# Steps of two attention rows instead of one in a fused window-attention and Fourier kernel

## The chip, the cores and the metric

The kernel runs on one core of one Trainium2 chip, in one launch, in float32. The metric is device time of one execution in microseconds (us).

Engines are named as the profile names them: PE is TensorE (matmuls), PEld its weight loads, DVE is VectorE, ACT ScalarE, POOL GpSimd, SP the engine that issues DMAs.

## The reference

Two layers are computed on 32 images of 56 x 56 tokens with 128 channels. Each adds its result to its input, and each works on a group norm of it (32 groups of 4 channels).

```python
def layer0(x):                       # shifted-window attention: window 7, shift 3, 4 heads of 32
    xs  = roll(x, (-3, -3));  win = windows_of_49_tokens(xs)
    q, k, v = split(win @ w_qkv.T)
    a   = softmax(q @ k.T * 32**-0.5 + rel_bias + shift_mask)
    return roll(unwindow(a @ v @ w_proj.T + b_proj), (3, 3))

def layer1(x):                       # Fourier layer: 32 modes along the width, 32 along the height
    xy = idct(einsum('bixy,ioy->boxy', dct(x, width )[..., :32], w0))
    xx = idct(einsum('bixy,ioy->boxy', dct(x, height)[..., :32], w1))
    return relu((xx + xy) @ W1 + b1) @ W2 + b2      # 128 -> 512 -> 128

x = x + layer0(group_norm(x))
x = x + layer1(group_norm(x))
```

(The text above is the reference in short form; names are shortened, the arithmetic is not.)

## The kernel before

An image has eight rows of windows, with eight windows of 49 tokens in each. The attention of one image runs beside the Fourier layer of the image before it and the feed-forward (the last two matmuls of the layer) of the one before that. The whole order of instructions on each engine is written by hand.

The parts of the kernel use TensorE in four tilings: full, 128x128 (q, k, transposes, projection, feed-forward), 128x64 (v, transforms, mix), 64x64 (scores, modes back), 64x32 (values). One cycle handles one row and goes through them:

```python
def attn_v(im, i, r):                # 128x64; 16 matmuls as the profile counts them
    pv = attn_bank()
    for w in (0, 2, 1, 3, 4, 6, 5, 7):
        nc.tensor.matmul(pv[...], lhsT=im.xw[i][...], rhs=im.w[:, 2*C:3*C], ...)
    nc.scalar.copy(v_sb[r % 3]..., pv)

def attn_scores(im, i, r):           # 64x64; 32 matmuls in the profile, then two adds on VectorE
    ps = [attn_bank(), attn_bank()]
    ...
    nc.vector.tensor_tensor(a[...], ps[hp][...], bm[...], ALU.add)

def attn_transpose(im, i, r):        # full
    for hf in range(2):
        pt = attn_bank()
        ...                          # four transposes into the bank
        if hf: nc.scalar.copy(aT[:PW, :, :PW], src)
        else:  nc.vector.tensor_copy(aT[:PW, :, :PW], src)

def attn_values(im, i, r):           # 64x32; 64 matmuls in the profile; reads aT and v
    po = [attn_bank(), attn_bank()]
    ...                              # then bias adds po -> oT, on VectorE and ScalarE

# [cut: statistics, transforms, mix, modes back, feed-forward]

for cycle in ...:                    # one row a cycle
    full_first(cycle, norm)          # transposes of row r-2, q and k of row r, feed-forward in, divide of row r-1
    if (cycle - CONV_BEGIN) % NWR != 3:
        quarters(cycle)              # scores of row r, modes back
        attn_max(cycle)
        half_columns(cycle)          # v of row r, transforms or mix
        eighths(cycle)               # values of row r-2
    else:                            # the same in another order
        ...
    full_last(cycle, norm)           # feed-forward out, exp of row r, projection of row r-2
```

## Time and profile before

| | before |
|---|---|
| median of 3 runs | 3698.61 us (3693.87 to 3700.42) |
| TensorE busy | 98% of the span |
| time per image in the steady part | 112.7 us |

How to read the views. The *page* gives busy time per engine, and the chain of work that ended last. The *waits of TensorE* list what it stood idle for: the line that waited, the releaser, the sum in us, how often, and the longest. "Issue" there is idle time in which it waited for nothing that the profile shows. The *timeline* gives start, duration, engine, line and instruction; a bracket at the end is the idle time before it and its releaser. A matmul record's end is modelled, so blocks are compared by their starts; and since idle time is counted from that modelled end, a row of the waits can give too little.

The line numbers move by one between the kernels. The parts on TensorE are:

```
                  before  after            before  after
image transposes  L259    L260   values     L444    L445
q / k             L321/8  L322/9 project    L486    L487
v                 L353    L354   transform  L595    L596
scores            L375    L376   mix        L629    L630
transposes        L419    L420   modes back L668    L669
                                 ff in/out  L711/31 L717/37
```

The waits of TensorE in the kernel before:

```profile
PE pa L259 <- DMA xl<-in_x_dram: 11.2, 2, 6.9
PE pa L375 <- DVE k L341: 8.3, 6, 1.8
...
PE pa L444 <- issue: 2.1, 4, 1.2
...
```

Nothing is large and no wait recurs for every image: there are 32 images, and the counts are 2, 6 and 4.

### The profile page before, as it was taken

Reading aid. Unit: us, or ns where it says so; the run is one execution under the profiler, and the core shown is the slowest. Engines: PE = TensorE matmul, PEld = TensorE weight load, DVE = VectorE, ACT = ScalarE, POOL = GpSimd, SP = SyncE. Lnnn points to the kernel's source line nnn. Section 1 sums busy time; section 2 is a strip of 40 time slices with the busy share of each in tenths; the row PEclk is TensorE's granted clock in tenths of the full one; section 3 lists DMA queues with packets and bytes.
Section 4 is the critical chain, followed back from the end, with each engine's and each line's share of the span. In section 5 each row is a group of like instructions: output and inputs, shape, how many; then the busy total and the mean of one; then the engine's idle time right before and its main releaser. Section 6 shows DMA issues by size and latency. Waiting matters only on the chain.

```text
span 3694.8 us, 139935 instructions
## 1 busy us (share of the span) xinstructions
PE 3628.2 (98%) x61440; PEld 2966.3 (80%) x61440; DVE 2185.3 (59%) x4577; ACT 2151.0 (58%) x3915; POOL 1372.0 (37%) x1421
## 2 busy tenths in 40 slices
PE   6899999999999999999999999999999999999998
PEld 5678888888888887888888888878888888888886
DVE  6655666655665556665556656556655566565641
ACT  4555566655656655566556566555665565565553
POOL 5333343333334333433333343334333333433321
PEclk9999999999999999999999999999999999999999
DMA  4333434343434334334334344343344343333332
GB/s 112 93 102 104 116 93 109 107 111 101 113 95 114 108 105 113 96 105 110 108 102 113 95 111 108 105 113 100 101 112 108 101 115 97 108 107 106 95 107 89
DMA packets 687777, 388.93 MB, mean 105 GB/s; under 512 B 40479, under 2 KB 658112, under 8 KB 686912
## 3 DMA queue, kind: packets, MB, share of 16 engines
q1 hardware_dynamic: 686557, 379.65, 37.6%
q8 instruction: 484, 7.93, 0.9%
q14 instruction: 125, 1.02, 0.1%
q10 hardware_dynamic: 611, 0.32, 0.0%
HBM read 218.29 MB, written 161.48 MB: 103 GB/s over the span
## 4 chain that ended last, share of the span: by engine, by line
PE 93%; DVE 4%; DMA 1%; SPq 1%; ACT 1%; issue 0%; POOL 0%; ACTq 0%; POOLq 0%; DVEq 0%
PE pc L731 21%; PE pc L711 18%; PE pa L353 7%; PE pc L629 6%; PE pc L595 6%; PE pa L375 6%; PE pa L419 5%; PE pa L486 5%; PE pc L668 5%; PE pa L328 5%; PE pa L444 4%; PE pa L321 4%; PE pa L259 2%; DVE st L270 1%; DVE a L383 1%; DVE mx L393 1%
## 5 line engine op out<-in xcount | busy, mean ns | idle before, releaser
L408 POOL TENSOR_TENSOR a<-a,rs 128x784 f32<-128x784 f32 x256 | 389.9, 1523 | 1231.0 <-DVE rs L407 962.6
L731 PE MATMUL pc<-wff,hid 128*128 128x128 f32 (+1 forms) x6400 | 778.6, 279 | 0.9 <-ACT hid L719 0.7
L731 PEld LDWEIGHTS pc<-wff,hid 128*128 128x128 f32 (+1 forms) x6400 | 731.1, 189 | 21.1 <-issue 2.1
L711 PE MATMUL pc<-xf,wff 128*128 128x512 f32 (+2 forms) x1792 | 713.1, 540 | 0.9 <-ACT z L637 0.9
L719 ACT ACTIVATE hid<-pc,b1sb 128x512 f32<-128x512 f32 (+2 forms) x896 | 536.6, 635 | 97.8 <-PE pc L711 94.2
L711 PEld LDWEIGHTS pc<-xf,wff 128*128 128x128 f32 x1792 | 337.0, 190 | 301.7 <-issue 229.5
L394 POOL TENSOR_TENSOR a<-a,mx 128x784 f32<-128x784 f32 x256 | 389.4, 1521 | 451.6 <-DVE mx L393 450.4
L740 DVE TENSOR_TENSOR res<-pc,res 128x512 f32<-128x512 f32 (+2 forms) x256 | 143.6, 571 | 597.0 <-issue 273.9
L427 ACT COPY aT<-pa 113x452 f32<-113x452 f32 x256 | 137.8, 538 | 457.6 <-PE pa L419 457.5
L274 POOL TENSOR_TENSOR xl<-xl,bproj 112x384 f32<-112x384 f32 (+1 forms) x256 | 291.9, 1142 | 248.7 <-PE pa L259 248.7
L383 DVE TENSOR_TENSOR a<-pa,bm 128x392 f32<-128x392 f32 x512 | 259.6, 550 | 199.3 <-PE pa L375 199.1
L341 DVE TENSOR_SCALAR k<-pa,heads,bqkv 128x392 f32<-128x392 f32 x246 | 168.6, 685 | 275.3 <-ACT k L333 275.3
L475 DVE TENSOR_SCALAR oT<-pa,bqkv 128x98 f32<-128x98 f32 (+2 forms) x768 | 171.0, 279 | 266.4 <-PE pa L444 266.4
L400 ACT ACTIVATE a<-a 128x784 f32<-128x784 f32 x256 | 223.1, 872 | 168.9 <-POOL a L394 168.5
L360 ACT COPY v<-pa 128x512 f32<-128x512 f32 x256 | 152.9, 597 | 278.4 <-PE pa L353 278.4
L701 POOL TENSOR_TENSOR res<-res,b2sb 128x512 f32<-128x512 f32 (+2 forms) x256 | 263.5, 1035 | 101.4 <-DMA res<-scr 91.3
L375 PEld LDWEIGHTS pa<-k,q 64*64 64x64 f32 x8192 | 184.0, 132 | 137.8 <-DVE rs L407 68.2
L353 PE MATMUL pa<-wn,xw 128*64 128x128 f32 x4096 | 281.8, 280 | 3.7 <-DVE a L383 3.7
L353 PEld LDWEIGHTS pa<-wn,xw 128*64 128x64 f32 x4096 | 219.8, 137 | 51.6 <-issue 17.2
L393 DVE TENSOR_REDUCE mx<-a 128x16 f32<-128x784 f32 x256 | 247.6, 967 | 5.7
L405 DVE TENSOR_REDUCE sm<-a 128x16 f32<-128x784 f32 x256 | 245.9, 961 | 4.9 <-ACT a L400 4.9
L419 PE MATMUL pa<-ident,a 113*113 113x113 f32 x2048 | 248.2, 264 | 0.7 <-POOL a L408 0.7
(89 smaller groups left out, 5896.8 us busy)
## 6 DMA issues: line engine op xcount, KB each, us to landing
zscr<-z SPq DMA_DIRECT2D x512, 112.0 KB
htok<-scr SPq DMA_DIRECT2D x256, 196.0 KB
zT<-zscr SPq DMA_DIRECT2D x192, 256.0 KB
res<-scr SPq DMA_DIRECT2D x160, 256.0 KB
out_dram<-res SPq DMA_DIRECT2D x128, 256.0 KB
scr<-xl SPq DMA_DIRECT2D x128, 224.0 KB
xl<-in_x_dram SPq DMA_DIRECT2D x32, 784.0 KB
xl<-in_x_dram SPq DMA_DIRECT2D x32, 672.0 KB
```

Of the source, the lines that this page charges most:

```text
L274: nc.gpsimd.tensor_tensor(piece, piece, bproj.unsqueeze(1).to_broadcast([TC, n1 - n0, C]), ALU.add)
L353: nc.tensor.matmul(pv[hs, j * C : (j + 1) * C], lhsT=im.xw[i][:, w * WT : w * WT + JP], rhs=im.w[:, 2 * C : 3 * C], start=True, stop=True,)
L375: nc.tensor.matmul(ps[hp][HALVES[e], pr * 2 * WT : (pr + 1) * 2 * WT], lhsT=q[cs, w * WT : w * WT + JP], rhs=k_sb[cs, :, w], start=True, s ...
L383: nc.vector.tensor_tensor(a[:, 2 * hp : 2 * hp + 2, :, 0:WT].rearrange("p u w j -> p w u j"), ps[hp][:, :RT].rearrange("p (w u j) -> p w u ...
L393: nc.vector.tensor_reduce(mx, a3, axis=AX.X, op=ALU.max)
L394: nc.gpsimd.tensor_tensor(a3, a3, mx.unsqueeze(2).to_broadcast([P, 2 * NWR, WT]), ALU.subtract)
L408: nc.gpsimd.tensor_tensor(a3, a3, rs.unsqueeze(2).to_broadcast([P, 2 * NWR, WT]), ALU.mult)
L419: nc.tensor.transpose(pt[:PW, h * P : h * P + PW], a[:PW, h, 2 * hf : 2 * hf + 2].rearrange("p w j -> p (w j)")[:, :PW], ident[:PW, :PW],)
L701: nc.gpsimd.tensor_tensor(res[:m, c0:c1], res[:m, c0:c1], b2sb[:m].unsqueeze(1).to_broadcast([m, c1 - c0, C]), ALU.add,)
L711: nc.tensor.matmul(ph[:, :n], lhsT=wff1[:, f * P : (f + 1) * P], rhs=xff[:, t0 : t0 + n], start=True, stop=True,)
L719: nc.scalar.activation(hf[:, :n], ph[:, :n], AF.Relu, bias=b1sb[:, f : f + 1])
L731: nc.tensor.matmul(pf[:m, c * C : (c + 1) * C], lhsT=im.hid[f][:, c * P : c * P + m], rhs=wff2[:, f], start=(f == 0), stop=(f == NF - 1),)
```

## The change

Its intent: two rows of attention per step, so that blocks of one tiling stand together and TensorE changes its tiling five times per two rows instead of eight. For that, the softmax of a row is a step (two rows) long, the transposes stand one step after the scores, the width modes are transformed back before the height modes, and the feed-forward has eight even groups in place of seven uneven ones. q, k and the transposed scores get further buffers; the buffers of the scores go from three to two.

```diff
-FF_GROUPS = (HB, HB, HB, HB, 320, 256, HB)
-FF_AT = (7, 8, 9, 10, 12, 13, 14)
+FF_GROUPS = (3 * P,) * 7 + (7 * JP,)
-CONV_BEGIN = NWR + 2
+CONV_BEGIN = NWR // 2 + 1
 [cut: buffers; k_sb[r % 2], q_sb[r % 2], a_sb[r % 2]; im.aT[i]; width copied, height added]
-    def full_first(cycle, norm):
-    def half_columns(cycle):
-    def quarters(cycle):
-    def eighths(cycle):
-    def full_last(cycle, norm):
+    def step(g):
+        prev, cur, b, i = rows(g - 1), rows(g), *divmod(g, STEPS)
 [cut: groups 6 and 7 of the next image; first part of its norm]
+        for im, d in conv:
+            if d >= FF_BEGIN:
+                ff_in(im, 2 * (d - FF_BEGIN))
+        for im, j, r in prev:
+            if once("divide", r):
+                attn_divide(r)
+        sums = []
+        for im, j, r in rows(g - 2):
+            if once("sums", r):
+                sums.append(attn_sums(im, j))
+                next(sums[-1])
+        for im, j, r in cur:
+            attn_qk(im, j, r, False)
+        if norm:
+            next(norm)
+        for k in sums:
+            next(k)
 [cut: first half of the statistics, loads]
+        for im, d in conv:
+            if d >= FF_BEGIN:
+                ff_out(im, 2 * (d - FF_BEGIN))
+                ff_in(im, 2 * (d - FF_BEGIN) + 1)
+        for im, d in conv:
+            if d == 0:
+                next(im.stats)
+        if norm:
+            next(norm)
+        if i == STEPS - 2:
+            groups((0, 1, 2))
+        for im, j, r in prev:
+            attn_transpose(im, j, r)
+        for im, j, r in prev[:1]:
+            attn_values(im, j, r)
+        for k in range(2):
+            for im, d in conv:
+                if d in (2, 3):
+                    modes_back(im, d == 2, k)
+        for im, j, r in cur:
+            attn_scores(im, j, r)
 [cut: modes_back of groups 2 and 3; maxima; transforms and mix]
+        for im, j, r in cur:
+            attn_v(im, j, r)
+        for im, j, r in prev[1:]:
+            attn_values(im, j, r)
+        for im, j, r in cur:
+            attn_exp(r)
+        for im, d in conv:
+            if d >= FF_BEGIN:
+                ff_out(im, 2 * (d - FF_BEGIN) + 1)
+        for im, j, r in prev:
+            attn_project(im, j)
 [cut: groups 3 to 5 of the next image; last part of its norm]
```

An image takes four such steps. I call the one with d = 0 the statistics step, the one with the next image's groups 0 to 2 the group step, and the one with the next image's norm the norm step.

## The prediction

> **What bounds the kernel now.** I read the page first (busy shares, slices, chain), then the busy time of each engine in the steady part, then the waits of TensorE, and last the timeline of TensorE, block by block.
>
> From the page and from the windows view (us of the window, then PE, PEld, DVE, ACT, POOL busy, clock):
>
> ```profile
> PE 3628.2 (98%) x61440; PEld 2966.3 (80%) x61440; DVE 2185.3 (59%) x4577; ACT 2151.0 (58%) x3915; POOL 1372.0 (37%) x1421
> ...
> PE 93%; DVE 4%; DMA 1%; SPq 1%; ACT 1%; issue 0%; POOL 0%; ACTq 0%; POOLq 0%; DVEq 0%
> ...
> 130.00:3500.00 3370.00, 3353.98 (x57453) 2748.83 (x57454) 2040.36 (x4257) 2000.43 (x3646) 1278.06 (x1316) 1.00 0.39 106
> ```
>
> TensorE is busy 98% of the span and 99.5% of the steady part, at full clock; it carries 93% of the chain. In its wait list nothing exceeds 11.2 us (the first image's load); all waits for another engine together come to some 55 us, nearly all in the first 130 us and the last 90. So the time is the sum of TensorE's work, and only two things can move it: less TensorE time, or a new wait of TensorE.
>
> A busy engine is not an engine at its peak, so I looked at how long the same block takes before different successors (timeline: start, duration, what):
>
> ```profile
> 1812.58 0.82 PE L328 MATMUL pa<-xw,wn 128*128 128x392 f32 x2
> 1813.24 3.60 PE L711 MATMUL pc<-xf,wff 128*128 128x512 f32 x8
> 1816.77 0.90 PE L375 MATMUL pa<-k,q 64*64 64x98 f32 x32
> 1817.60 1.09 PE L353 MATMUL pa<-wn,xw 128*64 128x128 f32 x16
> 1818.53 1.80 PE L595 MATMUL pc<-dct_h,htok 112*64 112x64 f32 x56
> ...
> 1841.39 0.90 PE L375 MATMUL pa<-k,q 64*64 64x98 f32 x32
> 1842.12 1.71 PE L668 MATMUL pc<-idcth,zT 64*64 64x112 f32 x64
> ...
> 1886.90 1.09 PE L353 MATMUL pa<-wn,xw 128*64 128x128 f32 x16
> 1887.92 0.81 PE L444 MATMUL pa<-aT,v 49*32 49x49 f32 x64
> ```
>
> Read starts, not durations (ends are modelled). The 32 score matmuls (64 rows x 64 columns) take 1817.60-1816.77 = 0.83 us when a block of another tiling follows, and 1842.12-1841.39 = 0.73 us when one of the same tiling follows. The 16 value projections (128x64) take 0.93 us before the transform of the same tiling and 1.02 us before the 49x32 block. So **a change of tiling costs about 0.10 us**, with no gap that the idle column would show.
>
> [...]
>
> **The change part by part.**
>
> *Tiling changes.* Before, each row of attention passes through full array, 64x64, 128x64, 64x32 (in one phase in another order): four changes a row, eight per two rows. Afterwards a step of two rows goes full array, 64x32 (values of the first row), 64x64, 128x64, 64x32, full array: five. Counted over the whole instruction order of TensorE, with each matmul put to its tiling, there are 1110 changes before and 726 after: 384 fewer. The sum is 384 x 0.10 = **38 us less** (1.0%), all of it on the path, since TensorE is the path. Per image of 113.2 us (from one image load's issue to the next) that is 12 x 0.10 = 1.2 us.
>
> *TensorE's other work.* Counts of transposes, projections, scores, values, transforms, mixes are equal. The feed-forward goes from seven groups (five of 512) to eight (seven of 384, one of 448): the same 3136 columns and the same 100 second-stage matmuls an image; 4 more wide matmuls, at a few ns each of fixed cost. Zero. The 64-token rest, with its two changes of tiling, stays.
>
> *Other engines.* Width now comes first and is copied out half by ScalarE, half by VectorE; height is added by VectorE alone. VectorE gains 128 copies of about 0.6 us (L684's mean 596 ns), 75 us, to 61%; ScalarE loses about as many. VectorE's load sits in the step that adds height: 2.4 divide + 2.4 sums + 1.4 keys + 1.2 transposes out + 1.7 values + 4.5 height + 2.0 scores + 1.9 maxima + 2.4 residuals and projection = about 20 us in a step of some 25 us. Laid beside TensorE's order, the bank that the value projection needs comes free about 0.9 us ahead. No wait, but thin.
>
> *The softmax.* Transposes now come one step after the scores, and within the step behind two feed-forward inputs, one output and two rows of queries and keys: 2 x 2.58 + 2.69 + 2.63 = 10.5 us. The divide needs two sums and reciprocals on VectorE (2 x 1.22) and two products on GpSimd (2 x 1.52), about 5.5 us after the step begins. Hidden.
>
> *What the shorter distance exposes.* The first row's values now come right behind the transposes: TensorE needs 16 x 0.099 = 1.6 us for both rows, and the copy of the first quarter (615 ns on VectorE) must be done by then. Usually it is. Not where VectorE has something ahead of it:
> - In the step that begins the Fourier part, the group statistics stand just ahead of the copies:
>
> ```profile
> 1898.77 0.33 PE L537 MATMUL pa<-tot,gmean 112*128 112x64 f32 x2
> ...
> 1900.13 0.55 POOL L566 TENSOR_TENSOR rstd<-ve,mhalf 128x1 f32<-128x1 f32 x1 [7.78 <-DVE ve L562]
> 1900.71 0.16 DVE L568 SCALAR_TENSOR_TENSOR shift<-ms,rstd 128x1 f32<-128x1 f32 x1 [0.66 <-POOL rstd L566]
> ```
>
> From the matmul to the end of shift it is 1900.87-1898.77 = 2.1 us; with the copy 2.75 us. TensorE gets there in 0.13 + 1.6 + 0.1 = 1.8 us. A wait of about **0.9 us**.
> - In the next step three window groups are transposed just ahead: three copies on ScalarE (0.49, behind the last relu, 0.6), three statistics on VectorE (0.56 each) and then the copy: 0.6 + 0.5 + 1.0 + 0.6 + 0.6 = 3.3 us against 1.24 + 1.6 + 0.1 = 2.9. About **0.4 us**.
> - In the norm step: 0.45 to ve, 0.75 for GpSimd's power with its hand-over, 0.2 for nb, then the copy, 2.0 against 1.9. About **0.1 us**.
>
> That is 1.4 us an image, x 31 = **43 us more**, if nothing hides it and the durations laid end to end are right to half a microsecond.
>
> *Ends.* In the first steps without feed-forward the softmax chain of two rows (about 10 us) stands against some 7 us of TensorE work; before, the same stretch (95 to 136 us) lost some 10 us in waits. At the end the transposing loads get a longer distance; before lost some 6 us there. I count both as zero.
>
> Sum: 3698.6 - 38 + 43 = 3704. Durations laid end to end overstate a chain (neighbours overlap by some 0.05 us in the timeline), so I take a fifth off the waits and name 3695.
>
> **The rivals.**
> 1. *The full gain of 38 us (3660).* For it: every wait above sits within half a microsecond of vanishing, and the order looks fitted around TensorE. Against it: the statistics chain has no room at all.
> 2. *VectorE becomes the bound in the height step.* For it: 20 us of work in 25, in order. One more microsecond late and the projection, the next step's divide and the transposes all slip: 2 us x 31 = 60 us, 3760. Against it: on average it is busy only 61%.
> 3. *GpSimd or the loads hold the softmax.* The residual add stands ahead of the divide in GpSimd's queue; if its load came late, the transposes would wait. Against it: the order of the load queue shows each residual load issued a group ahead, and TensorE's waits for loads before are 17 us in all. Were it true, 3 us a step x 124 would give over 4000; I don't believe it.
>
> **Range and chances.** The gain is firm to 10%: it is a count times a cost seen three times. The waits are uncertain by their whole size, 0 to 90 us. That gives 3655 to 3745. Two per cent is 74 us: faster needs a gain twice what the changes of tiling hold, slower needs rival 2 or 3. Faster 0.04, same 0.91, slower 0.05.
>
> **What would show it.** In the timeline after, a score block of 32 followed by another of 32 should take 0.73 us, and TensorE's busy time should fall by about 38 us. The wait list of TensorE should show the value block (L445) waiting for VectorE's copies some 60 times, about 1 us and 0.4 us, and nothing for loads. If those waits are absent, rival 1; if the value projection or the projection waits for the score or height adds, rival 2; if the transposes wait for GpSimd, rival 3. I am wrong in substance if TensorE's busy time does not fall.

## The result

The changed kernel took 3780.35 us (median of 4 runs, 3775.74 to 3781.98) against 3696.38 us before (4 runs, 3693.87 to 3700.42). The ratio is 1.0224, with a 95% interval of 1.0206 to 1.0242: **slower by 2.2%**, 84 us.

From the page of the changed kernel, and from its windows view (the steady part; columns as in the prediction):

```profile
PE 3612.5 (96%) x61696; PEld 3055.2 (81%) x61696; DVE 2280.0 (60%) x4739; ACT 2155.6 (57%) x3913; POOL 1366.0 (36%) x1453
...
PE 84%; DVE 7%; ACT 4%; issue 3%; SPq 1%; DMA 1%; POOL 0%; ACTq 0%; DVEq 0%; POOLq 0%
```

```profile
130.00:3500.00 3370.00, 3246.43 (x56175) 2757.30 (x56176) 2072.46 (x4284) 1949.61 (x3545) 1237.53 (x1313) 1.00 0.40 103
```

TensorE's busy time did fall, by 15.7 us (3628.2 to 3612.5), but it is now idle for 123.6 us of the steady 3370 (3370 - 3246.43), where it was idle for 16.0. VectorE, ScalarE and "issue" have taken shares of the chain from it (84%, where it had 93%). So the kernel did not get more work; it got waits. They are these (waits of TensorE):

```profile
PE pa L445 <- DVE aT L430: 40.2, 61, 1.4
PE pa L376 <- issue: 27.8, 37, 1.6
PE pc L717 <- DVE res L746: 19.8, 29, 0.7
...
PE pa L445 <- issue: 7.4, 5, 3.5
PE pc L737 <- issue: 7.3, 6, 1.7
...
```

There are three kinds of them. The first is the one predicted: values waiting for VectorE's copy of the transposes, twice an image. The second is "issue", 51.8 us over all lines, against 3.4 before. The third is the feed-forward's input waiting for a residual add on VectorE, once an image.

The statistics step of an image near the middle shows the first two (timeline; the copy on VectorE is L430):

```profile
1941.97 1.79 PE L420 MATMUL pa<-ident,a 113*113 113x113 f32 x16
1943.74 0.16 DVE L569 SCALAR_TENSOR_TENSOR shift<-ms,rstd 128x1 f32<-128x1 f32 x1 [0.66 <-POOL rstd L567]
1943.81 1.16 DVE L430 COPY aT<-pa 113x452 f32<-113x452 f32 x2
1944.58 0.80 PE L445 MATMUL pa<-aT,v 49*32 49x49 f32 x64 [0.82 <-DVE aT L430]
1945.31 1.55 PE L376 MATMUL pa<-k,q 64*64 64x98 f32 x53
...
1947.95 0.55 PE L376 MATMUL pa<-k,q 64*64 64x98 f32 x11 [1.08 <-issue]
```

The copies begin only when `shift` is written, and the values stand for 0.82 us: that is the chain the prediction laid out. Then the scores stop after 53 of 64 matmuls, in the middle of a block, for 1.08 us. Their operands q and k are long there (the last of them was written by 1938.14 us), and the other 53 had them too.

The norm step shows the third kind:

```profile
1882.20 2.10 PE L717 MATMUL pc<-xf,wff 128*128 128x384 f32 x6
1884.97 0.91 PE L717 MATMUL pc<-xf,wff 128*128 128x384 f32 x2 [0.67 <-DVE res L746]
```

The second feed-forward group of the step needs four banks; the fourth is the one that holds the output of the first group until VectorE has added the residual, and that add stands behind both rows' sums on VectorE.

**What "issue" is.** The list of DMA queues has one for instructions:

```profile
q8 instruction: 485, 7.95, 0.9%
```

That is 485 packets in 7.95 MB, 16.4 KB each. The trace records 124,249 instructions of TensorE (61,696 matmuls, as many weight loads, and 857 of its sequencer): 124,249 / 485 = 256.2 a packet. In the kernel before it is 123,886 / 484 = 256.0. I take it from this that the queue carries TensorE's program, in blocks of 256 instructions. I then set each stall of TensorE against the last instruction fetch that began before its end (my own evaluation of the trace, us; not a view of the profile):

```
stall of the changed kernel           times   its end, counted from the   its end, counted from the
                                              fetch's start               end of the fetch's packet
scores, "issue" (L376)                 37     2.18 to 2.83                1.19 to 1.59
all "issue" of TensorE                 66     2.18 to 3.47
values waiting for the copy (L445)     61     no relation (3.02 to 18.49)
```

All 37 stalls of the scores end at nearly the same moment of a fetch, and so do the other 29; waits for a copy show no such relation. Counted along TensorE's recorded instructions, those of the sequencer included, all 66 also stand at the same place of a block of 256: the count of instructions ahead of them, less whole blocks, is 193 or 194. So I take it that TensorE has used up one block and waits for the next; the scores' stalls then say that a fetch is of use some 2.4 us after it starts. No two fetches of this trace start less than 3.25 us apart, which is 256 / 3.25 = 79 instructions a us. On average TensorE takes 123,392 / 3778.7 = 33 instructions a us, far fewer than 256 in 2.4 us. But the step puts its densest blocks side by side: values are 128 instructions (matmuls and weight loads) in 0.73 us, and the two rows of scores that now follow are 128 more in 1.4 us, together 120 a us. In the kernel before, each of these blocks had a block of fewer and longer matmuls on at least one side: feed-forward input ahead of most scores, feed-forward output behind most values.

**Where the time went, part by part.** Each TensorE instruction's time is taken as the distance to the next one's start, summed over 28 images and divided by 28 (my own evaluation of the traces, us an image):

```
                     before  after   change
transposes             6.44   8.25   +1.81   wait for the copies +1.42, changes of tiling now behind them +0.38
scores                 6.24   7.63   +1.39   "issue", and waits for banks (below)
ff in                 21.69  22.12   +0.43   bank wait +0.95, fewer changes of tiling -0.52
ff out, modes back,
  values, transform   41.94  42.94   +1.00
project                6.12   6.26   +0.14
q and k               11.12  10.54   -0.58   no change of tiling behind them any more
mix, v                14.88  14.50   -0.38
image transp., norm    4.29   3.86   -0.43
image                112.73 116.11   +3.38
```

The split of "ff in" is from experiments below, where the wait is gone and the part takes 21.17. Over 29 images the steady part loses 3.38 x 29 = 98 us; the first image interval (97.1 to 92.2 us) and the part after the last statistics (115.8 to 109.9) give back 11. That is the measured 84 to within a few us.

So the expected saving is visible (q, k, feed-forward input, v, mix: -1.48 us an image, -43 us in 29), and some 150 us stand against it (1.81 + 1.39 + 0.95 + 1.00 + 0.14 = 5.29 us an image), nearly all of it waits and slower blocks; 11 us (0.38 x 29) are changes of tiling that moved behind the transposes.

**The scores, start by start.** Their "issue" row has 27.8 us; counted from start to start, less the usual step, these stalls take 34 us in the 28 images. A second wait has no row, since it hides in the modelled end of the matmul before it: in the steps with transforms, the 37th of the 64 matmuls starts 0.15 us after VectorE has written the last piece of oT of the first row's values, in nearly every one of the 56 blocks (10% to 90%: 0.147 to 0.148). It needs the bank that this empties. Such a block takes 1.78 us (median), and 1.58 in the experiment below in which v stands between: 0.2 us twice an image, 12 us in 29.

### The profile page after: what moved, and what is told of

The parts are those of the page before. It is cut to its first block, busy times and chain, and to the rows that moved or that the text cites. A ratio compares the mean times of both kernels' runs of the same rounds, so it can differ in the third digit from the quotient of the medians.

```text
span 3778.7 us, 140104 instructions
## 1 busy us (share of the span) xinstructions
PE 3612.5 (96%) x61696; PEld 3055.2 (81%) x61696; DVE 2280.0 (60%) x4739; ACT 2155.6 (57%) x3913; POOL 1366.0 (36%) x1453
## 3 DMA queue, kind: packets, MB, share of 16 engines
q8 instruction: 485, 7.95, 0.9%
## 4 chain that ended last, share of the span: by engine, by line
PE 84%; DVE 7%; ACT 4%; issue 3%; SPq 1%; DMA 1%; POOL 0%; ACTq 0%; DVEq 0%; POOLq 0%
PE pc L737 18%; PE pc L717 15%; PE pc L630 6%; PE pc L596 6%; PE pa L354 6%; PE pa L376 5%; PE pa L487 5%; PE pa L445 5%; PE pc L669 4%; PE pa L329 4%; PE pa L322 4%; PE pa L420 3%; ACT hid L725 2%; PE pa L260 2%; DVE st L271 1%
## 5 line engine op out<-in xcount | busy, mean ns | idle before, releaser
L725 ACT ACTIVATE hid<-pc,b1sb 128x384 f32<-128x384 f32 (+1 forms) x1024 | 600.3, 587 | 610.4 <-PE pc L717 557.2
L737 PE MATMUL pc<-wff,hid 128*128 128x128 f32 x6400 | 783.3, 278 | 8.0 <-issue 7.3
L737 PEld LDWEIGHTS pc<-wff,hid 128*128 128x128 f32 x6400 | 745.4, 190 | 52.6 <-issue 8.7
L717 PE MATMUL pc<-xf,wff 128*128 128x384 f32 (+1 forms) x2048 | 727.0, 496 | 19.8 <-DVE res L746 19.8
L746 DVE TENSOR_TENSOR res<-pc,res 128x384 f32<-128x384 f32 (+1 forms) x288 | 148.1, 523 | 375.6 <-PE pc L737 208.5
L707 POOL TENSOR_TENSOR res<-res,b2sb 128x384 f32<-128x384 f32 (+1 forms) x288 | 270.4, 944 | 263.3 <-DMA res<-scr 254.9
L604 ACT ACTIVATE y<-pc,rstd 128x448 f32<-128x448 f32 x256 | 167.5, 655 | 195.6 <-PE pc L596 189.7
L384 DVE TENSOR_TENSOR a<-pa,bm 128x392 f32<-128x392 f32 x512 | 256.2, 558 | 36.1 <-PE pa L376 31.4
L376 PE MATMUL pa<-k,q 64*64 64x98 f32 x8192 | 231.4, 248 | 32.7 <-issue 27.8
L445 PE MATMUL pa<-aT,v 49*32 49x49 f32 x16384 | 208.7, 212 | 49.5 <-DVE aT L430 40.2
L445 PEld LDWEIGHTS pa<-aT,v 49*32 49x32 f32 x16384 | 174.5, 105 | 89.1 <-ACT aT L428 50.8
## 6 DMA issues: line engine op xcount, KB each, us to landing
zT<-zscr SPq DMA_DIRECT2D x192, 256.0 KB
```

The lines of the kernel that those rows point to most:

```text
L376: nc.tensor.matmul(ps[hp][HALVES[e], pr * 2 * WT : (pr + 1) * 2 * WT], lhsT=q[cs, w * WT : w * WT + JP], rhs=k[cs, :, w], start=True, stop ...
L384: nc.vector.tensor_tensor(a[:, 2 * hp : 2 * hp + 2, :, 0:WT].rearrange("p u w j -> p w u j"), ps[hp][:, :RT].rearrange("p (w u j) -> p w u ...
L445: nc.tensor.matmul(po4[u][h * HD : (h + 1) * HD, 2 * f + e], lhsT=v[ks, 2 * f + e, h * HD : (h + 1) * HD], rhs=im.aT[i][f][ks, h, e * JP : ...
L707: nc.gpsimd.tensor_tensor(res[:m, c0:c1], res[:m, c0:c1], b2sb[:m].unsqueeze(1).to_broadcast([m, c1 - c0, C]), ALU.add,)
L717: nc.tensor.matmul(ph[:, :n], lhsT=wff1[:, f * P : (f + 1) * P], rhs=xff[:, t0 : t0 + n], start=True, stop=True,)
L725: nc.scalar.activation(hf[:, :n], ph[:, :n], AF.Relu, bias=b1sb[:, f : f + 1])
```

## The experiments

My theory after seeing the trace had three causes, each repairable by order alone: copies late behind statistics (A), a supply of instructions too slow for dense neighbours (B), sums ahead of the residual on VectorE in the norm step (C). The main rival was that VectorE's work is simply late wherever it stands, so that every repair makes another wait.

Three calls were made; the medians of before in them were 3694.45 (7 runs), 3698.92 (7) and 3696.98 us (9). All kernels gave correct results. Differences between kernels are taken between their ratios, times 3697 us.

### Copies ahead of the statistics (cause A)

```diff
+        for im, j, r in prev:
+            attn_transpose(im, j, r)
         for im, d in conv:
             if d == 0:
                 next(im.stats)
 [cut: norm, groups 0 to 2]
-        for im, j, r in prev:
-            attn_transpose(im, j, r)
```

> The changed kernel with the group statistics, the norm's second half and the three window groups moved behind the transposes of the probabilities, so that the copies of the transposed probabilities come first on VectorE. Theory (the copies stand behind those chains): the value block's waits for VectorE's copies (40.2 us, 61 times in the changed kernel) fall below 5 us and the time falls by 35 to 43 us, from 3780 to about 3742. Rival (the supply of instructions to TensorE, or the next bank, is the real floor of the step): the waits vanish but come back as issue waits or as waits of the scores, and the time falls by less than 15 us.

Measured: 3743.03 us (3739.98 to 3749.34), ratio 1.0135 [1.0120, 1.0150], so 33 us faster than the changed kernel. The wait for aT is all but gone (0.8 us, once) and the transposes are back at 6.44 us an image. But other waits of TensorE have come:

```profile
PE pa L376 <- DVE oT L476: 24.6, 60, 0.6
...
PE pa L376 <- issue: 15.6, 26, 1.4
```

The scores now wait, twice an image, for banks that VectorE empties into oT late, behind the statistics. Cause A is confirmed, with a net worth of 33 us rather than the 40.2 us of the wait's row: part of it returned one block later, in the wait for banks of the scores, which is long enough here to have a row.

### Second half of the sums behind the feed-forward in the norm step

```diff
         for k in sums:
-            next(k)
+            if not norm:
+                next(k)
 [cut: feed-forward out and in]
+        for k in sums:
+            if norm:
+                next(k)
```

> The changed kernel with, in the norm step alone, the second half of the group sums moved behind the feed-forward output, so that VectorE adds the first feed-forward residual earlier and its bank comes free in time. Theory (the fourth first-stage feed-forward matmul waits for that bank in the norm step): the waits L717 for DVE res (19.8 us, 29 times) vanish, the block of 8 goes from 3.52 us to 2.58 us, the time falls by 20 to 28 us to about 3755. Rival (VectorE is late in that step whatever the order): the wait moves to the copies of the transposed probabilities in the norm step and the time stays within 8 us of 3780.

Measured: 3832.02 us (3827.66 to 3844.02), ratio 1.0379 [1.0359, 1.0399]: 57 us *slower* than the changed kernel. The wait that it was to remove is gone (feed-forward in 22.12 to 21.17 us an image), but in this place the sums stand right before the norm's small instructions and the copies:

```profile
PE pa L445 <- DVE aT L430: 63.0, 89, 1.4
PE pa L420 <- DVE ve L300: 30.4, 29, 1.1
```

The values now wait three times an image instead of twice, and the transposes wait for the norm. Part of the loss is the clock, which the four runs show at 0.988 to 0.990 where those of all other kernels but one (both rows of values together, below: 0.987 to 0.990) have 0.994 or more. In this trace it was granted at half in 17 stretches of 3.4 or 6.8 us, the first 200 us and the last 110 left out (3 in the changed kernel), and the same kinds of matmuls took 26 us longer in them than outside (4.7 us in the changed kernel; an evaluation of the traces' clock records). Each of the 17 began right after 3.4 us in which TensorE had stood idle for 1.5 to 2.5 us; the changed kernel's three followed 1.6, 2.3 and 3.4 us. What sets off such a stretch isn't shown: 3.4 us with 1.6 us idle (from 1026.0 us of the changed kernel's trace) were not followed by one. This was the rival's case and it held here: a wait moved is not a wait removed. It leaves open whether a better place exists.

### v between the dense blocks (cause B)

```diff
         for im, j, r in prev[:1]:
             attn_values(im, j, r)
+        for im, j, r in cur:
+            attn_v(im, j, r)
 [cut: modes back, scores, transforms, mix]
-        for im, j, r in cur:
-            attn_v(im, j, r)
```

> The changed kernel with the value projection (32 matmuls in 1.85 us, few instructions) moved in between the first row's values and the scores: one more change of tiling in most steps (124 x 0.10 = 12 us more). Theory (TensorE runs out of instructions where values and scores, 128 instructions in 0.73 us and 128 in 1.46 us, follow each other): issue waits fall from about 52 us to under 20, and the score block of 64 before transforms goes from a median of 1.77 us to 1.45 us since the output copies of the first row get time: sum -45 -19 +12, about 3728. Rival (the issue waits are semaphore waits that the profile doesn't name): issue waits of the scores stay at 28 us and more, time 3760 to 3790.

Measured: 3746.77 us (3744.12 to 3755.14), ratio 1.0147 [1.0132, 1.0162]: 28 us faster than the changed kernel, less than expected. The work is the same, and it has 93 more changes of tiling (819 against 726 in the trace), 7 to 9 us at 0.08 to 0.10 us each. Scores fell from 7.63 to 5.96 us an image.

```profile
PE pa L445 <- DVE aT L430: 40.4, 61, 1.4
...
PE pa L445 <- issue: 8.5, 16, 1.2
```

The copy wait is untouched, as it should be. The "issue" of the scores is 0.4 us (27.8 before this edit); some of it moved to the second row's values, which had stood behind v and now stand behind transforms and mix. The fall of the scores (1.67 us an image, 48 us in 29) is larger than their 27.8 us of "issue". The rest is what the row leaves out of those stalls, and the banks: scores right behind the first row's values take banks that have just been used and must be emptied into oT, and v in between gives them time. The starts in the changed kernel's trace show that wait (above); this edit alone would not tell the two effects apart. Feed-forward output now waits 9.4 us for VectorE, a row that the changed kernel doesn't have, which is part of why the gain is less than expected.

### Both rows of values together (cause B, the other way)

This is the first experiment (copies ahead of the statistics) with the values of both rows behind v: four changes of tiling a step. It needs a fourth buffer for v; to make room, the mask borrows a tile and `tot` is left with one buffer.

```diff
-        for im, j, r in prev[:1]:
-            attn_values(im, j, r)
 [cut]
-        for im, j, r in prev[1:]:
+        for im, j, r in prev:
             attn_values(im, j, r)
```

> As e1, and the values of both rows at the end of the step behind the value projection: four changes of tiling per two rows in place of five (12 us less), a fourth buffer for v. Theory of the instruction supply: the scores now follow slow full-array work, so their issue waits vanish, and with them the wait for the first row's output banks (19 us); but the two rows' values are 256 instructions in 1.46 us, so issue waits of the value block appear, 10 to 40 us in all. Time 3670 to 3710. Rival (issue waits are not a matter of density): issue waits stay with the scores, 28 us; time about 3700 to 3710.

Measured: 3780.55 us (3771.04 to 3790.6), ratio 1.0232 [1.0207, 1.0258]. It has the fewest changes of tiling of all (601 in the trace) and no copy wait, and is as slow as the changed kernel. The time expected was missed; the direction of cause B was not:

```profile
PE pa L446 <- issue: 53.8, 33, 5.2
PE pc L738 <- issue: 14.9, 10, 3.2
PE pc L718 <- DVE res L747: 13.1, 20, 0.7
PE pa L446 <- ACT v L362: 12.0, 27, 1.4
```

The values (L446 here) are now 256 instructions in 1.46 us, and TensorE stands 53.8 us in the middle of that block, up to 5.2 us at once. Apart makes the stall go, together makes it grow: I take cause B as shown. What isn't seen is how many instructions TensorE holds ahead. The values also wait 12.0 us for ScalarE's copy of v, which now stands right ahead of them.

Two things go with these stalls. The long ones fall where data transfers fill the DMA engines: in the 2.5 us before the fetch began that ended it, the 16 engines had packets under way throughout for each of the 14 longest stalls (2.46 to 5.18 us), against a mean share of 0.40 in the steady part. That the fetch waits behind data fits this, but no run tests it. And the clock fell, as in the second experiment: 17 stretches at half clock, counted in the same way, each right after 3.4 us in which TensorE had been idle for 1.1 to 3.2 us, in which the same kinds of matmuls took 29 us longer. The window around the stall of 4.4 us (us of the window; last three: clock, DMA share, GB/s):

```profile
449.00:456.00 7.00, 4.03 (x21) 3.91 (x22) 0.67 (x3) 1.94 (x3) 0.00 (x0) 0.51 1.01 179
```

### A and B repaired together

On top of the copies ahead of the statistics, v of the first row goes between its values and the scores, and v of the second row stays ahead of its values: six changes of tiling a step.

```diff
+        for im, j, r in cur[:1]:        # behind the first row's values
+            attn_v(im, j, r)
 [cut]
-        for im, j, r in cur:
+        for im, j, r in cur[1:]:
             attn_v(im, j, r)
```

> The changed kernel with both repairs: copies of the transposed probabilities first (as e1), and the value projection split, the first row's half between the first row's values and the scores, the second row's half ahead of the second row's values: six changes of tiling per two rows. Theory (waits for copies, and the supply of instructions, are separate causes): the transposes' share goes from 8.25 to 6.44 us an image as in e1 and the scores' from 7.63 to about 6.0 as in e3, without e3's 0.5 us more in the values, since no dense block stands beside another; six changes cost 0.4 us an image more. 116.1 - 1.8 - 1.6 + 0.4 = 113.1 us an image, time about 3695. Rival (one floor behind both, say VectorE or ScalarE late by a fixed amount in each step): time stays at 3725 or more, as in e1 alone.

Measured: 3706.81 us (3704.08 to 3710.1), ratio 1.0027 [1.0012, 1.0042], 12 us over what I expected. Against the changed kernel it is 1.97 points or 73 us; A alone gave 0.89 points and B alone 0.77, so together they give more than their sum. I put that down to v between the blocks, which also lets oT be emptied before the scores want its banks: the scores' wait for oT, 24.6 us with A alone, has no row of 0.6 us or more here.

### Both halves of the sums behind mix (cause C, on top)

```diff
 [the sums of the norm step are skipped above]
+        for k in sums:                  # behind transforms and mix, ahead of v of the second row
+            if norm:
+                for _ in k:
+                    pass
```

> As e5, with the group sums of the norm step (both halves) moved behind the mixing of the modes, where VectorE has time (mask and totals made smaller so that the squares get a buffer of their own). e2 moved only the second half, by a little, and lost 52 us. Theory (in the norm step VectorE and ScalarE are late for the fourth bank of the second feed-forward group because eight or so small works stand ahead): the wait of the first-stage feed-forward (about 0.45 us an image, 18 to 20 us in all) vanishes, time 15 to 20 us below e5. Rival (another engine, ScalarE's relus behind five window copies, sets that wait): within 5 us of e5.

The squares of the sums get a buffer of their own for this, and the mask and `tot` make room as above. (In the changed kernel the squares waited for no buffer, so the buffer itself can't be the gain.)

Measured: 3695.78 us (3687.65 to 3703.32), ratio 0.9990 [0.9970, 1.0010]: 11 us less at the median than the one above, not the 15 to 20 expected, and equal to before. In the version above the profile put this wait down to ScalarE's relus (`hid`), not to VectorE:

```profile
PE pc L717 <- ACT hid L725: 18.7, 27, 0.7
```

The row is gone here. Part of the sums, the squares, runs on ScalarE, so the sums are the cause on either engine; which of the two comes last is not separated. Feed-forward in fell from 22.14 to 21.17 us an image, the size expected. A new wait took some of it, in the projection:

```profile
PE pa L488 <- DVE oT L477: 11.0, 12, 2.0
```

### A change of tiling by itself

These two put one small matmul ahead of each row's key matmul in the kernel *before*, 256 in all: once on the full array, where its neighbours are, and once on a 64x64 tile, which adds two changes of tiling each. The result isn't read, so the output stays correct.

```diff
         pk = attn_bank()
+        nc.tensor.matmul(pk[:, 448:449], lhsT=ident, rhs=ident[:, 0:1], ...)              # full
+        nc.tensor.matmul(pk[:JP, 448:449], lhsT=ident[:JP, :JP], rhs=ident[:JP, 0:1], ...) # or this: 64x64
```

> The kernel before, with one more matmul of one column on the full array in front of each row's key matmul (256 in all): no change of tiling. [...]28 to 36 us more than before.

> The same with the extra matmul on a 64x64 tile: two changes of tiling each, 512 in all. Theory (a change costs 0.10 us): [...]55 to 75 us more than before, clearly more than e7 although the matmul itself is smaller. Rival (changes of tiling cost nothing of themselves, what was read was the tail of the last block): not more than e7.

Measured: full 3754.33 us, ratio 1.0153 [1.0138, 1.0169]; tiled 3793.78 us, ratio 1.0264 [1.0249, 1.0279]. That is 57 and 98 us more than before, where I expected 28 to 36 and 55 to 75: I had undersized the matmul's own cost. It is about 57 us / 256 = 0.22 us for this matmul of one column on the full array (two records in the profile), where 28 to 36 us would be 0.11 to 0.14. The difference between the two is 39.5 us at the medians, for 512 changes of tiling, although the tiled matmul is smaller: at least 39.5 / 512 = 0.08 us for a change. The timelines of the full and of the tiled one:

```profile
1822.73 0.84 PE L321 MATMUL pa<-xw,wn 128*128 128x392 f32 x2
1823.41 0.28 PE L328 MATMUL pa<-ident 128*128 128x1 f32 x2
1823.55 0.90 PE L329 MATMUL pa<-xw,wn 128*128 128x392 f32 x2
```

```profile
1815.85 0.84 PE L321 MATMUL pa<-xw,wn 128*128 128x392 f32 x2
1816.62 0.27 PE L328 MATMUL pa<-ident 64*64 64x1 f32 x2
1816.82 0.93 PE L331 MATMUL pa<-xw,wn 128*128 128x392 f32 x2
```

From q's start to the small matmul's it is 0.68 us without a change of tiling and 0.77 with one: 0.09 us, and again without idle time in any column. The term of the prediction for a change of tiling stands.

### The sums in a place where nothing follows (causes A, B and C)

The two last runs put the norm step's sums behind the second row's values. On top of the version that equalled before:

```diff
-        for k in sums:                  # no longer ahead of v of the second row
 [cut]
         for im, j, r in prev[1:]:
             attn_values(im, j, r)
+        for k in sums:
+            if norm:
+                for _ in k:
+                    pass
```

> e6 once more, with one move: the norm step's sums stand behind the second row's values on VectorE's queue instead of ahead of them. In e6 the projection waited 11.0 us (12 times) for the values' copy oT, which stood behind the sums. If that wait comes from the sums alone, it goes and nothing takes its place: 8 to 12 us less than e6, i.e. 0.997 of before (about 3686 when before is 3697). Rival: the sums then stand ahead of the next step's divide on VectorE (3 us late), the transposes wait for GpSimd's products, and the time stays at e6's, 0.999 to 1.002.

Measured: 3685.11 us (5 runs, 3681.5 to 3692.11), ratio 0.9964 [0.9951, 0.9978]. It is the fastest kernel: 0.4% under before and 2.6 points under the changed kernel. The wait of the projection went from 11.0 to 3.7 us and nothing took its place. Waits of TensorE, from a profile that fell on the slowest of the five runs:

```profile
PE pa L446 <- issue: 6.9, 12, 1.2
PE pc L738 <- issue: 6.8, 5, 3.3
...
PE pa L488 <- DVE oT L477: 3.7, 3, 2.0
```

### Cause C alone

The same move in the changed kernel, with nothing else altered in the order (the squares of the sums get their own buffer; the mask borrows a tile and `tot` has one buffer).

> The changed kernel with only the norm step's sums moved behind the second row's values (the transposes, the copies and the order on TensorE stay as in the changed kernel; the squares of the sums get a buffer of their own, the mask borrows a tile). It measures the term that the prediction lacked, the fourth bank of the norm step's second feed-forward group, which waits 19.8 us (29 times) for a residual on VectorE behind the sums. Theory: that wait goes, the feed-forward input falls from 22.14 to 21.2 us an image, and nothing follows in its place: 25 to 30 us less than the changed kernel, about 1.015 of before (3752 when before is 3697). Rival (what e2 showed when the sums were moved only as far as behind the feed-forward): VectorE's work is late wherever it stands in this step, the copies or the divide wait instead, and the time stays within 10 us of the changed kernel's, 1.020 or more.

Measured: 3755.07 us (4 runs, 3747.52 to 3760.04), ratio 1.0155 [1.0140, 1.0170]: 26 us less than the changed kernel, within what was expected. Feed-forward in is 21.17 us an image. The wait for res is no longer in the list of waits, and the two others are near what they were:

```profile
PE pa L446 <- DVE aT L431: 38.6, 61, 1.7
PE pa L377 <- issue: 26.5, 35, 1.8
```

The experiment in which only the second half of the sums was moved, and only by two blocks, had given +57 us. So the rival is right about the place and wrong as a rule: VectorE has room in this step, behind the second row's values.

## Why the prediction was wrong

The prediction named 3695 us, with a range up to 3745; 3780 us is outside it. By its own steps:

**TensorE is the bound, and only less work or a new wait can move the time.** Right, and the result is the second case.

**384 changes of tiling at 0.10 us.** Right in kind and size: 0.08 to 0.10 us each by three measurements (the score blocks of the prediction, the two timelines above, the two times above), so 31 to 38 us; the parts that lost their changes fell by about 43, and the transposes gained 11 by changes that moved behind them.

**The copies of the transposes, 43 us, some 60 waits.** Right: 40.2 us, 61 waits, in the two steps with 0.9 and 0.4 us (0.89 and 0.52 from start to start, less the usual step: 41 us in 29 images). The third of its three places, the norm step with 0.1 us, did not appear: TensorE came later to it, behind the wait for the residual. It appeared in the second experiment (89 waits for copies in place of 61), where that wait was gone and half the sums stood right ahead of the copies.

**"TensorE's other work. Counts ... are equal. ... Zero."** This is the first step that failed. Equal counts in another order aren't equal time. (The few ns for more wide matmuls were right: in the trace before, one of 512 columns takes 429 ns to the next one's start and one of 256 takes 216, which leaves 3 ns.) With values beside scores, 120 instructions a us, "issue" went from 3.4 to 51.8 us: by the experiments on cause B, TensorE's supply of instructions. The prediction looked at the order only for tilings and operands. The view that would have warned is the queue list with its instruction packets, together with the count of instructions in a block over the block's time.

**"What the shorter distance exposes."** The second failure. The list followed only the operands of the values, and it took one wait per step. It left out who empties the banks: the fourth bank of the second feed-forward group in the norm step (0.95 us an image; 26 us by the experiment on it alone), and the banks of the second row's scores (12 us from start to start). VectorE was laid beside TensorE's order for the height step, and the norm step was the one without slack.

**The ends, zero.** Wrong by 11 us, in favour of the change.

**The fifth taken off the waits.** It wasn't borne out: the wait was 40.2 us by its row and 41 by the starts, near the 43 unshaded, and the sum lacked others.

**The rivals.** The full gain didn't come. VectorE as the bound of the height step didn't come: the waits that the prediction gave for it, of v and of the projection for VectorE, are 2.8 and 2.3 us in all. The residual adds on GpSimd and their loads held the transposes for 0.6 us in all. The nearest was the second, in another step and by 20 to 26 us, not 60. None had the supply of instructions in it, so a chance of 0.05 for slower was too low.

**What would show it.** The test "TensorE's busy time should fall by about 38 us" gave 16: the right sign and half the size. The score blocks of two rows take 1.35 us ahead of modes back (0.68 for 32, below the 0.73 foretold) and 1.78 ahead of transforms (0.89), where the wait for banks is.

**Off the path.** VectorE gained 94.7 us (2185.3 to 2280.0), not 75, and ScalarE lost nothing (2151.0 to 2155.6), since its relus of the eight groups take 63.7 us more (536.6 to 600.3). The 596 ns that the prediction used for VectorE's copies is ScalarE's time. Nothing of the result hangs on these.

The sum, with all terms as the parts table has them, times 29: -43 (q and k, feed-forward in, v, mix) - 12 (image transposes and norm) + 52 (transposes: 41 of waits for copies, 11 of changes of tiling) + 40 (scores: some 35 of "issue" and 12 for banks, less fewer changes) + 28 (cause C) + 29 (feed-forward out, modes back, values, transform, where rows of "issue" have 20.9 us) + 4 (projection) - 11 (ends) = 87 us. Measured: 84.

Undoing shows the same: A, B and C undone singly are worth 0.89, 0.77 and 0.69 points, 2.35 in sum; the whole loss is 2.24, and all three together give 2.60. What still keeps the best version from the full saving is seen in part. It makes six changes of tiling a step, not five (850 in the trace against 726), and it has some 19 us of "issue" in all rows. In its trace (the slowest of the five runs) an image takes 112.77 us, as before (112.73): values are 6.72 us (5.98 before) and v 8.11 (7.59), so what it has gained there is in the first and last images. Whether an order exists with five changes and without those stalls stays open.

## What to carry to other kernels

When blocks are reordered on a bound TensorE, ask three things of every new pair of neighbours, not one: are the operands there, who empties the bank it writes and what stands ahead of that on its engine, and how many instructions per us the two blocks take together (here 120, with fetches that began at least 3.25 us apart, 79 a us). A saving that comes from putting like with like put dense with dense here; a block of few, long instructions between them cost one change of tiling more in most steps (93 in all, 7 to 9 us) and made the kernel 28 us faster. And a small job on a helper engine is placed behind the last thing in the step that TensorE waits for, since moving it a little way may only move the wait: the second half of the sums cost 57 us in one place, and both halves gained 26 us in the other. Waits can go with more than their own time: in two experiments the clock was granted at half in 17 stretches each, every one right after 3.4 us of which TensorE had stood idle for 1.1 us or more, and the same kinds of matmuls took 26 and 29 us longer in them.
